# Seven outer products of a Strassen stage: summed in accumulating DMAs instead of on VectorE and GpSimd

## The chip, the cores and the metric

One core of a Trainium2 chip. The metric is device time in microseconds (us) of one execution of the whole program. Five engines work side by side and wait for each other through semaphores: TensorE (PE, with its weight loads as PEld), VectorE (DVE), ScalarE (ACT), GpSimd (POOL) and SyncE (SP, which here only issues DMAs). POOL can issue DMAs as well. Each engine takes its instructions strictly in order: an instruction that waits holds everything behind it on the same engine.

## The reference

Input x has shape (4, 512, 512), all in float32. Two residual blocks follow each other:

```
h = layernorm(x)
i, f, g = h Wi^T, h Wf^T, h Wg^T
gate = sigmoid(f);  v = silu(i) * (1 - gate)
o[t] = gate[t] * o[t-1] + v[t]                     # scan over the 512 tokens
o = o / rms(o) * gnorm_w * g * sigmoid(g)
x = x + layernorm(o Wo)
h = layernorm(x)
hidden = fwht(silu(h W1^T) * (h W3^T))             # width 2048, Walsh-Hadamard
x = x + layernorm(hidden W2^T)
```

The change touches only the last block, the product with W1 and W3, and there only for the batches 2 and 3.

## The kernel before

The Hadamard transform is folded into W2 early in the kernel. Nearly all products are made by one step of Strassen's scheme in Winograd's form: 2x2 blocks, seven products instead of eight. The seven are named P1, P2, P6, P5, P7, P3, P4 in the order in which they are made (`ORDER`, line 33). They go to three PSUM banks: X takes P1, then P6, P7 and P4 on top of it, Y takes P2, Z takes P5 and then P3 on top. Because a bank is summed further, PE may start P6 only when P1 has been read out of X, P7 only after P6 was read, P4 only after P7 was read, and P3 only after P5 was read.

Batches 0 to 3 pass through the attention block, and batches 0 and 1 through the feed-forward block, in this way. The two last batches are treated as a pair (`PAIR = 2, 3`, `ffn_pair`, lines 834 to 914): their product with W1 and W3 gets two levels of the scheme. An outer step stands for one of the seven outer products; it consists of the seven inner products, which I call leaves. A leaf is two matmul calls (line 879) of 128x128 by 128x256 each. The outer order is P1, P2, P6, P7, P5, P4, P3 (`OUTER`). There are four groups g = 0 to 3 of the hidden width, so 4 x 7 outer steps of 7 leaves.

Each leaf is read from PSUM at once (lines 887 to 892), as a 128x512 piece of a 128 x 2048 accumulator in SBUF, `q`, with urgent priority. In the kernel before an outer product is summed as it leaves PSUM. `q0` starts as P1 (ACT copies the fresh pieces, line 889; the other three are added by DVE, line 892); `q1` = q0 + P2, `q0` += P6, `q3` = P7 (fresh pieces again by ACT), `q2` = q0 + P5, all of them by DVE additions that read PSUM. In the step of P5, POOL adds q3 into q0 (line 894) and q2 into q3 (line 896), eight additions of 128x512. Last, q0 += P4 and q2 += P3 by DVE. The four sums are then the four blocks of the result: `hidden` (lines 849 to 865) takes one of them, applies Silu to its first half on ACT (line 852) and multiplies the halves on DVE into the tiles `ht` (line 860, two per call). `combine_left` (lines 158 to 163) then makes the scheme's four sums of each `ht` on POOL.

The product of `ht` with W2, "down" (`ffn_out`, line 684), of one group is made between the leaves of the next group (lines 903 to 907: 56 single matmul calls per group, spread from the fourth leaf to the 48th). The last group's is made after all leaves, in one go, and ends in the normalization and the stores.

What sets the order: PE and SP take their instructions in the order of the source. DVE, ACT and POOL get an order from a scheduler, which goes by priorities and its own estimates; `tc.high_priority` raises a piece of work. `load_leaf_w` (line 813) has SP load the weights of the step three ahead, and POOL makes four sums of them too (`wl`, lines 158 to 163). SP also loads 2 x 896 KB of W2 tiles (`load_down_pair`, line 186) at the start of each group. PSUM has eight banks.

Of the kernel before, what the change touches and what calls it, by code (L numbers as in the profile page):

```python
# [11 lines left out]
F32 = mybir.dt.float32  # L12
AF = mybir.ActivationFunctionType
ALU = mybir.AluOpType
P = 128
# [29 lines left out]
def kernel(  # L45
# [14 lines left out]
    nc = tc.nc  # L60
    B, T, D = x.shape
# [12 lines left out]
    xpool = ctx.enter_context(tc.tile_pool(name="x", bufs=3))  # L74
    stream = ctx.enter_context(tc.tile_pool(name="stream", bufs=5))
    stream2 = ctx.enter_context(tc.tile_pool(name="stream2", bufs=4))
    work = ctx.enter_context(tc.tile_pool(name="work", bufs=1))
# [10 lines left out]
    def bank(name):  # L88
        return psum.tile([P, 2, H], F32, tag="ps", name=name)
# [65 lines left out]
    def combine_left(t, eng, steps=(0, 1)):  # L155

        if 0 in steps:
            eng.tensor_add(t[:, S1], t[:, A21], t[:, A22])  # L158
            eng.tensor_sub(t[:, S2], t[:, S1], t[:, A11])
        if 1 not in steps:  # L160
            return
        eng.tensor_sub(t[:, S3], t[:, A11], t[:, A21])
        return eng.tensor_sub(t[:, S4], t[:, A12], t[:, S2])  # L163
# [85 lines left out]
    def behind(what):  # L249


        return tc.issue_after(read[what].ins)
# [555 lines left out]
        for make, (k, what) in zip(makes, places[first:]):  # L808
            beside.setdefault(k, []).append(partial(step, make, what))

    leaf_w = {}

    def load_leaf_w(n):

        g, k = divmod(n, len(OUTER))
        if g == NU // NS:
            return
        a = OUTER[k][1]
        t = stream.tile([P, 2, 7, P], F32, tag="w", name=f"wl_{g}_{a}")
        for w, name in enumerate(("w1", "w3")):  # L820
            for i in range(NS):
                nc.sync.dma_start(
                    out=t[:, w, 2 * i : 2 * i + 2],
                    in_=saved[name, NS * g + i][:, a].rearrange("p (c f) -> p c f", c=2),
                )
        combine_left(t.rearrange("p w s f -> p s w f"), nc.gpsimd)
        leaf_w[n] = t
# [6 lines left out]
    def ffn_pair(g, down):  # L834

        total, start = len(down), 3
        given = 0
        q = {}
        first_of = {"P1": (0, None), "P7": (3, None), "P2": (1, 0), "P5": (2, 0)}
        to_of = {"P1": 0, "P2": 1, "P6": 0, "P7": 3, "P5": 2, "P4": 0, "P3": 2}  # L840

        def accumulator(k):
            pool, tag, bufs = (work, "d", 2) if k == 0 else (xpool, "x", 3)
            q[k] = pool.tile([P, 2, 2, T], F32, tag=tag, name=f"q{k}_{g}", bufs=bufs)

        def part(k, i, j):
            return q[k][:, :, i, ts(j, H)]

        def hidden(k, h, j):

            d, b = q[k], PAIR[j]
            nc.scalar.activation(d[:, 0], d[:, 0], AF.Silu)  # L852
            for n in range(NS):
                m = NS * g + n
                if (b, m) not in hts:
                    hts[b, m] = work.tile(
                        [P, 7, H], F32, tag="ht", name=f"ht_{b}_{m}", bufs=4
                    )
                t = hts[b, m]
                nc.vector.tensor_mul(  # L860
                    t[:, h : h + 3 : 2],
                    d[:, 0, n].rearrange("p (t f) -> p t f", t=2),
                    d[:, 1, n].rearrange("p (t f) -> p t f", t=2),
                )
            return [hts[b, NS * g + n] for n in range(NS)]

        for step, (outer, _, right, _, _) in enumerate(OUTER):
            load_leaf_w(7 * g + step + AHEAD)
            w, x = leaf_w.pop(7 * g + step), xq[right]
            to, base = to_of[outer], None  # L870
            if outer in first_of:
                to, base = first_of[outer]
                accumulator(to)
            ps = {}
            for s, (what, a, bb, which, first) in enumerate(ORDER):
                if first:
                    ps[which] = bank(f"{which}_u{g}_{step}")
                for k in range(2):
                    nc.tensor.matmul(  # L879
                        ps[which][:, k, :], w[:, k, a, :], x[:, bb, :],  # L880
                        start=first and k == 0, stop=True, skip_group_check=True,
                    )
                i, j = {"P1": (0, 0), "P5": (1, 1), "P6": (0, 1), "P2": (0, 0),
                        "P7": (1, 1), "P3": (0, 1), "P4": (1, 0)}[what]
                fresh = what in ("P1", "P6", "P5", "P4")
                y = part(to, i, j)
                with tc.high_priority(offset=URGENT):
                    if fresh and outer in ("P1", "P7"):
                        read["copy"] = nc.scalar.copy(y, ps[which])  # L889
                    else:  # L890
                        z = part(base, i, j) if fresh and base is not None else y
                        last = nc.vector.tensor_add(y, ps[which], z)  # L892
                if outer == "P5" and fresh:
                    nc.gpsimd.tensor_add(part(0, i, j), part(0, i, j), part(3, i, j))
                if outer == "P5" and what in ("P2", "P7", "P3", "P4"):
                    nc.gpsimd.tensor_add(part(3, i, j), part(3, i, j), part(2, i, j))
                if acts and s in (0, 2, 4):
                    with behind("copy"):
                        acts.popleft()()
                if sums and what in ("P2", "P7", "P3"):  # L900
                    with tc.issue_after(last.ins):
                        sums.popleft()()
                leaf = 7 * step + s + 1
                want = total if leaf >= 48 else total * max(leaf - start, 0) // (48 - start)
                while given < want:
                    down.popleft()()
                    given += 1
            if outer == "P4":
                hidden(1, 0, 0)
                for t in hidden(0, 1, 0):  # L910
                    combine_left(t, nc.gpsimd)
        hidden(3, 1, 1)
        for t in hidden(2, 0, 1):
            combine_left(t, nc.gpsimd)

    def load_wo():
# [304 lines left out]
    for b in range(2):  # L1221
        late = {}
        for m in range(NU):
# [8 lines left out]
            if b == 0 and m in LOW:  # L1232
                p, what, k = LOW[m]
# [56 lines left out]
    for g in range(NU // NS):  # L1290
        load_down_pair(g)
        ffn_pair(g, deque(down))
        down = [
            part
            for b in PAIR
            for part in ffn_out(b, g, True)
        ]
# [36 lines left out]
```

## Time and profile before

| | |
|---|---|
| median of 3 runs | 791.99 us (791.94 to 792.12) |
| the profiled execution | 792.25 us |
| its span in the profile | 790.5 us (so 1.75 us lie around it) |
| PE busy in the span | 776.3 us, 98% |
| DVE, ACT, POOL busy | 564.2, 246.9, 245.5 us |
| granted clock of PE | 0.996 |
| leaves (line 879): first and last matmul record | 490.2 and 755.9 us |
| DVE additions to q (line 892) | 164, mean 0.69 us |
| ACT copies to q (line 889) | 32, mean 0.58 us |
| POOL sums of q (lines 894 and 896) | 32, mean 1.27 us |

The span is the time from the first to the last recorded instruction. A group in the profile is all instructions of one line, engine and operation; the idle time given with it is the engine's own, just before these instructions, with what ended it. The pair stage begins at 490 us, and its four groups at 490, 554, 622 and 690 us; the last "down" runs from 756 to 780 us.

### The profile page before, as it was taken

How to read it: one execution, taken by the hardware profiler on the slowest of the kernel's cores; microseconds unless marked ns; L12 is line 12 of the kernel's file. 1: busy time of each engine (PE TensorE's matmuls, PEld its weight loads, DVE VectorE, ACT ScalarE, POOL GpSimd, SP SyncE). 2: the span in 40 equal slices, each digit the busy share in tenths (PEclk: the TensorE clock that was granted, in tenths of full speed). 3: DMA queues.
4: the chain of work that ended last, by engine and by line, in shares of the span. 5: the costliest groups of instructions: out<-in, count | busy, mean ns of one | idle time of the engine just before them, and what ended most of it. 6: DMA issues, size and time to landing. Idle time of an engine off the chain costs nothing.

```text
span 790.5 us, 10222 instructions
## 1 busy us (share of the span) xinstructions
PE 776.3 (98%) x3608; PEld 670.1 (85%) x3608; DVE 564.2 (71%) x1093; ACT 246.9 (31%) x348; POOL 245.5 (31%) x319
## 2 busy tenths in 40 slices
PE   9999999999999999999999999999999999999994
PEld 7888788888888888888888888888788888888884
DVE  6789889799789774477455459868755655765676
ACT  4374754543436212344223412011321200111112
POOL 2111202112213110001001005088947646672452
PEclk9999999999999999999999999999999999999998
DMA  9997445776997982538246736341521412141012
GB/s 296 398 340 299 156 198 180 218 258 244 339 336 289 340 325 102 160 150 347 94 187 200 267 78 221 131 122 33 195 80 54 157 53 58 49 166 54 1 53 108
DMA packets 78148, 144.93 MB, mean 183 GB/s; under 512 B 6160, under 2 KB 55952, under 8 KB 77712
## 3 DMA queue, kind: packets, MB, share of 16 engines
q1 hardware_dynamic: 68032, 96.82, 38.1%
q0 software_dynamic: 9344, 46.14, 14.9%
q10 hardware_dynamic: 720, 1.31, 0.4%
q8 instruction: 29, 0.48, 0.2%
q14 instruction: 23, 0.19, 0.1%
HBM read 97.06 MB, written 47.19 MB: 182 GB/s over the span
## 4 chain that ended last, share of the span: by engine, by line
PE 88%; DVE 5%; DMA 2%; POOL 1%; issue 1%; SPq 0%; ACT 0%; POOLq 0%; DVEq 0%
PE X_f L517 13%; PE X_po L684 13%; PE X_u L879 11%; PE X_a L517 10%; PE Z_po L684 7%; PE Z_f L517 6%; PE Z_u L879 5%; PE Z_a L517 5%; PE X_y L624 3%; PE Y_f L517 3%; PE Y_po L684 3%; PE Y_a L517 3%; PE Y_u L879 3%; PE Z_y L624 2%; DMA w2p<-in_W_dram 1%
## 5 line engine op out<-in xcount | busy, mean ns | idle before, releaser
L684 PE MATMUL X_po<-w,ht 128*128 128x256 f32 x512 | 132.1, 379 | 0.1
L517 PE MATMUL X_f<-xt_f,w 128*128 128x256 f32 x512 | 121.2, 380 | 0.1
L879 PE MATMUL X_u<-xq,wl 128*128 128x256 f32 x448 | 114.4, 381 | 2.3 <-ACT q L889 0.8
L517 PEld LDWEIGHTS X_f<-xt_f,w 128*128 128x128 f32 x512 | 96.8, 190 | 14.5 <-DVE d_f L492 0.5
L684 PEld LDWEIGHTS X_po<-w,ht 128*128 128x128 f32 x512 | 97.2, 190 | 13.7 <-DVE f L492 0.5
L879 PEld LDWEIGHTS X_u<-xq,wl 128*128 128x128 f32 x448 | 84.2, 190 | 17.1 <-issue 3.6
L892 DVE TENSOR_TENSOR q<-X_u,q 128x512 f32<-128x512 f32 x88 | 60.8, 691 | 42.6 <-PE X_u L879 41.7
L494 ACT COPY d_f<-X_f 128x512 f32<-128x512 f32 x48 | 28.0, 584 | 131.8 <-PE X_f L517 115.7
L684 PE MATMUL Z_po<-w,ht 128*128 128x256 f32 x256 | 66.4, 379 | 0.0
L492 DVE TENSOR_TENSOR f<-X_po,f 128x512 f32<-128x512 f32 x51 | 34.9, 685 | 36.9 <-PE X_po L684 36.9
L517 PE MATMUL Z_f<-xt_f,w 128*128 128x256 f32 x256 | 60.5, 379 | 0.0
L879 PE MATMUL Z_u<-xq,wl 128*128 128x256 f32 x224 | 57.6, 379 | 0.0
L684 PEld LDWEIGHTS Z_po<-w,ht 128*128 128x128 f32 x256 | 48.6, 190 | 6.8 <-DVE f L492 0.2
L517 PEld LDWEIGHTS Z_f<-xt_f,w 128*128 128x128 f32 x256 | 48.6, 190 | 6.6
L263 POOL TENSOR_TENSOR rs_f<-rs_f,power 128x2 f32<-128x2 f32 x16 | 13.4, 840 | 117.8 <-DVE nm_f L364 73.5
L852 ACT ACTIVATE q<-q 128x1024 f32<-128x1024 f32 x16 | 16.9, 1057 | 103.8 <-DVE q L892 58.2
L879 PEld LDWEIGHTS Z_u<-xq,wl 128*128 128x128 f32 x224 | 42.5, 190 | 6.0 <-DVE q L892 0.3
L892 DVE TENSOR_TENSOR q<-Z_u,q 128x512 f32<-128x512 f32 x48 | 33.1, 689 | 20.1 <-PE Z_u L879 19.5
L158 POOL TENSOR_TENSOR wl<-wl 128x256 f32<-128x256 f32 x28 | 21.3, 762 | 77.4 <-DMA wl<-s_w 70.2
L494 ACT COPY d_a<-X_a 128x512 f32<-128x512 f32 x36 | 21.1, 585 | 67.8 <-PE X_a L517 67.6
L889 ACT COPY q<-X_u 128x512 f32<-128x512 f32 x24 | 14.0, 584 | 89.4 <-PE X_u L879 76.8
L179 POOL DMA_DIRECT2D s_w<-w x24 | 13.1, 547 | 72.5 <-DVE w L163 56.9
(205 smaller groups left out, 1459.2 us busy)
## 6 DMA issues: line engine op xcount, KB each, us to landing
w<-s_w SPq DMA_DIRECT2D x32, 896.0 KB, 6.4
s_w<-w POOLq DMA_DIRECT2D x24, 896.0 KB, 6.9
wl<-s_w SPq DMA_DIRECT2D x112, 128.0 KB, 2.7
w<-in_W_dram SPq DMA_DIRECT2D x32, 256.0 KB, 6.4
wi<-s_wi SPq DMA_DIRECT2D x6, 896.0 KB, 9.3
wf<-s_wf SPq DMA_DIRECT2D x6, 896.0 KB, 5.4
wg<-s_wg SPq DMA_DIRECT2D x6, 896.0 KB, 6.3
w_h<-w2p POOLq DMA_DIRECT2D x8, 512.0 KB, 5.7
```

The source lines that it names most:

```text
L158: eng.tensor_add(t[:, S1], t[:, A21], t[:, A22])
L179: nc.gpsimd.dma_start(out=saved[key], in_=t)
L263: read["power"] = nc.gpsimd.tensor_tensor(r, r, power_t[:, 0:n], ALU.pow)
L492: read[what] = nc.vector.tensor_add(to, ps[which], to)
L494: read["copy"] = nc.scalar.copy(to, ps[which])
L517: nc.tensor.matmul(ps[:, n, :], w[:, a, c, :], xt[:, bb, c, :], start=first and n == 0 and c == 0, stop=c == 1, skip_group_check=True,)
L624: nc.tensor.matmul(ps[:, t, :], og[:, a, c, ts(t, P)], w[c][:, bb, :], start=first and t == 0 and c == 0, stop=c == 1, skip_group_check=True,)
L684: nc.tensor.matmul(ps[:, t, :], hts[b, m][:, a, ts(t, P)], w[m][:, W2[bb], :], start=first and k == 0, stop=m == ms[-1], skip_group_check= ...
L852: nc.scalar.activation(d[:, 0], d[:, 0], AF.Silu)
L879: nc.tensor.matmul(ps[which][:, k, :], w[:, k, a, :], x[:, bb, :], start=first and k == 0, stop=True, skip_group_check=True,)
L889: read["copy"] = nc.scalar.copy(y, ps[which])
L892: last = nc.vector.tensor_add(y, ps[which], z)
```

## The change

Every outer product but P3 is now written fresh to an accumulator of its own: ACT copies the four fresh leaves (P1, P6, P5, P4), DVE adds the other three onto them. P3 is added by DVE onto the buffer called q0, all seven leaves. There are five accumulators, allocated once, whose parts rotate between groups (`places`). The sums between accumulators are six DMAs per group (`gather`), issued by POOL with `accum_op=add`: each adds one whole accumulator of 128 x 2048 float32 (1 MB) to another in SBUF. In the notation "target += source" they are: q1 += q0 after P2's step, q0 += q4 after P6's, q3 += q0 after P7's, q0 += q2 and then q2 += q3 after P5's, q3 += q4 after P4's. The POOL additions of lines 894 and 896 are gone. `hidden` is called for q1 after P5's step, for q2 and q3 after P4's, and for q0 at the end. In the changed kernel the gather is line 849, Silu 866, the product into `ht` 874, the leaf's matmul 890, the ACT copy 900 and the DVE addition 902.

```diff
-        q = {}
-        first_of = {"P1": (0, None), "P7": (3, None), "P2": (1, 0), "P5": (2, 0)}
-        to_of = {"P1": 0, "P2": 1, "P6": 0, "P7": 3, "P5": 2, "P4": 0, "P3": 2}
-
-        def accumulator(k):
-            pool, tag, bufs = (work, "d", 2) if k == 0 else (xpool, "x", 3)
-            q[k] = pool.tile([P, 2, 2, T], F32, tag=tag, name=f"q{k}_{g}", bufs=bufs)
+        roles = {"P1": 0, "P2": 1, "P6": 4, "P7": 3, "P5": 2, "P4": 4, "P3": 0}
+        places = {0: 1, 1: 4, 4: 3, 3: 2, 2: 0}
+        if not q:
+            for k in range(5):
+                pool, tag, bufs = (work, "d", 2) if k in (0, 4) else (xpool, "x", 3)
+                q[k] = pool.tile([P, 2, 2, T], F32, tag=tag, name=f"q{k}", bufs=bufs)
+        else:
+            before = dict(q)
+            q.update({k: before[place] for k, place in places.items()})
+
+        def gather(to, part):
+            nc.gpsimd.dma_start(
+                out=q[to].rearrange("p n i t -> p (n i t)"),
+                in_=q[part].rearrange("p n i t -> p (n i t)"),
+                accum_op=ALU.add,
+            )
+
+        gathers = {
+            "P2": ((1, 0),), "P6": ((0, 4),), "P7": ((3, 0),), "P5": ((0, 2), (2, 3)),
+            "P4": ((3, 4),),
+        }
...
-            to, base = to_of[outer], None
-            if outer in first_of:
-                to, base = first_of[outer]
-                accumulator(to)
+            to = roles[outer]
...
-                    if fresh and outer in ("P1", "P7"):
+                    if fresh and outer != "P3":
                         read["copy"] = nc.scalar.copy(y, ps[which])
                     else:
-                        z = part(base, i, j) if fresh and base is not None else y
-                        last = nc.vector.tensor_add(y, ps[which], z)
-                if outer == "P5" and fresh:
-                    nc.gpsimd.tensor_add(part(0, i, j), part(0, i, j), part(3, i, j))
-                if outer == "P5" and what in ("P2", "P7", "P3", "P4"):
-                    nc.gpsimd.tensor_add(part(3, i, j), part(3, i, j), part(2, i, j))
+                        last = nc.vector.tensor_add(y, ps[which], y)
...
+            for pair in gathers.get(outer, ()):
+                gather(*pair)
+            if outer == "P5":
+                hidden(1, 0, 0)
             if outer == "P4":
-                hidden(1, 0, 0)
-                for t in hidden(0, 1, 0):
+                hidden(2, 1, 1)
+                for t in hidden(3, 1, 0):
                     combine_left(t, nc.gpsimd)
-        hidden(3, 1, 1)
-        for t in hidden(2, 0, 1):
+        for t in hidden(0, 0, 1):
             combine_left(t, nc.gpsimd)
```

More of the change, by code (lines that the diff above doesn't have):

```diff
@@ L809, in pair_beside @@
             beside.setdefault(k, []).append(partial(step, make, what))
-    leaf_w = {}
+    leaf_w, q = {}, {}
     def load_leaf_w(n):
```

## The prediction

> **What bounds the kernel now.** I read the page's busy times first, then its chain that ended last.
>
> ```profile
> span 790.5 us, 10222 instructions
> PE 776.3 (98%) x3608; PEld 670.1 (85%) x3608; DVE 564.2 (71%) x1093; ACT 246.9 (31%) x348; POOL 245.5 (31%) x319
> PE 88%; DVE 5%; DMA 2%; POOL 1%; issue 1%; SPq 0%; ACT 0%; POOLq 0%; DVEq 0%
> ```
>
> PE is the path. Whether anything the change relieves holds PE up is seen in the table of stretches, cut at the four groups of the pair stage (columns: stretch, its length, then busy time and instructions of PE, PEld, DVE, ACT and POOL, granted clock, DMA share, GB/s).
>
> ```profile
> 490.00:554.00 64.00, 63.10 (x287) 53.54 (x286) 50.59 (x82) 8.24 (x12) 41.09 (x48) 1.00 0.29 91
> 554.00:622.00 68.00, 67.32 (x310) 58.20 (x309) 42.74 (x69) 15.63 (x24) 47.50 (x60) 1.00 0.30 94
> 622.00:690.00 68.00, 67.22 (x312) 58.89 (x311) 41.62 (x64) 8.80 (x12) 41.95 (x52) 1.00 0.27 83
> 690.00:756.00 66.00, 66.00 (x307) 57.84 (x306) 40.92 (x63) 8.81 (x12) 33.11 (x40) 1.00 0.21 75
> ```
>
> PE is idle 0.90 + 0.68 + 0.78 + 0 = 2.4 us in the whole stage. That is about all that any relief of DVE and POOL can win. The waits of PE name 0.8 us for ACT's q and 0.5 us for DVE's q, those of PEld 1.7 us more for DVE's q, part of it beneath running matmuls.
>
> **What goes and what comes, by count.** Away: DVE additions of line 892 fall from 164 to 25 a group (three in each of six steps, seven in P3's), 100 in all: 64 x 0.69 = 44 us less on DVE. The POOL sums go: 32 x 1.27 = 41 us. Added: 64 ACT copies x 0.58 = 37 us, and 24 gathers, whose issue takes POOL some 0.55 us each (the row of its stores of the output), 13 us. All of this lies beside PE: ACT goes from 8.8 to about 18 of 66 us in a group. I count the sum as 0, and at best 2.2 us won. An ACT copy is also no slower than the addition it replaces (0.58 against 0.69), so PSUM banks come free no later while ACT's queue flows.
>
> **What the gathers cost is a chain of waits.** Take G as the time from the issue of one gather to the earliest issue of one that waits for it. In a group, q0 += q2, then q2 += q3, then q3 += q4 must follow one another: the second writes what the first reads, the third writes what the second reads. The first can go only when P5's step is read out. POOL waits in front of each, with `wl` and `ht` sums queued behind. Then Silu needs q3. I lay this on the trace of before, since PE's order of work is unchanged.
>
> ```profile
> 601.22 1.03 PE L879 MATMUL X_u<-xq,wl 128*128 128x256 f32 x4
> 621.08 1.89 PE L879 MATMUL X_u<-xq,wl 128*128 128x256 f32 x8
> 624.62 1.10 PE L879 MATMUL X_u<-xq,wl 128*128 128x256 f32 x4 [0.79 <-ACT q L889]
> ```
>
> These are PE's rows: the last leaf of group 1's P5 step, the last of its P3 step (first half of the 8), and a wait that is there already.
>
> *Groups 1, 2 and 3.* P5's last leaf ends at 602.25; ACT's copy (0.09 us later, 0.58 us) ends at 602.9; the first gather issues at 603.0 and the third lands at 603.0 + 3G. In the built program the first `ht` product of that block (line 874) stands in DVE's queue between P3's Z addition and P7's X addition. So DVE waits for the landing and Silu (1.06, line 852's row), multiplies (0.69), adds P7 (0.69), with 0.2 for hand-overs, and behind it wait the rest of the leaf additions, and PE, whose P4 leaf was due at 621.0: stall 603.0 + 3G + 2.6 - 621.0 = 3G - 15.4. The P4 gather's own input is ready at about 613, before 603 + 2G.
>
> *Group 0* has shorter steps. P5's last leaf ends at 537.4, first gather 538.1; here Silu stands in ACT's queue ahead of the copy of the next group's P1, and P6 of that step was due at 555.8: stall 538.1 + 3G + 1.06 + 0.58 + 0.2 - 555.8 = 3G - 15.9.
>
> *A second place* in groups 1 to 3: Silu of q1 stands in ACT's queue after P6's copy in step 3 of the group (outer P6), ahead of P5's copy, and waits for q1 += q0. In group 1 P2's step is read out at 573.6; Silu and copy with hand-overs add 1.8; P3's leaf, which sums onto P5's bank, is due at 580.0: stall G - 4.6. In group 0 Silu stands one copy later, where no leaf of that bank follows: 0.
>
> Sum: (3G - 15.9) + 3(3G - 15.4) + 3(G - 4.6), no term below 0.
>
> **G is not in the trace**; no DMA there adds. Three rows bound it, minimum, median and maximum from issue to landing: 256 KB stores from POOL (line 724), 896 KB stores (179), 1 MB loads (151), and the page's row of POOL's queue.
>
> ```profile
> DMA to landing us min/median/max: 2.0/3.4/7.5
> DMA to landing us min/median/max: 3.9/7.4/12.6
> DMA to landing us min/median/max: 4.7/4.9/5.0
> q0 software_dynamic: 9344, 46.14, 14.9%
> ```
>
> 46.14 MB in 14.9% of 790.5 us is 392 GB/s while packets run, so 1.05 MB takes 2.7 us and 256 KB 0.67; the fixed part is 2.0 - 0.67 = 1.33 us (check: 896 KB gives 3.7, the row's minimum is 3.9). From below: the addition is free, landing 4.0, G = 4.1. From above: two reads and a write one after the other, 1.33 + 3 x 2.7 = 9.4, G = 9.5. I take two transfers' worth, since source and target must both be read while the write can run beside them: 1.33 + 5.4 = 6.7, with 0.15 for POOL to wake, G = 6.9. It is also between the quiet (4.0) and the loaded (7.4, 896 KB median) rows.
>
> The Trainium skill, "Collectives: The Full Stack", the bandwidth ceiling in Part 3, speaks against this change: an add in the DMA costs no cycles, but needs two source reads, and halves the rate (62.28 against 32.35 GB/s, a ratio of 1.93). No run here shows it yet; with 1.93 in place of 2 the landing would be 6.5 and the stall some 3 us less. Its praise of such sums, that compute engines stay free, is what the table above makes worthless here: they are not the path.
>
> With G = 6.9: 4.8 + 3 x 5.3 + 3 x 2.3 = 27.6 us. The forecast is 792.25 + 27.6 = 819.9, say 820 (made against the profiled execution, which stands 0.26 above the median of its three runs). With G = 6 it would be 14, with G = 8.2 about 47: its own range is 806 to 840.
>
> Other waits I cost at nothing: POOL's `wl` sums behind the gathers. In group 1 with G = 6.9 POOL is through with both waits and 16 `ht` sums of some 0.76 us by about 36 us after P5's end, while the weights that follow are needed some 50 us after it (a stalled PE needs them later still). If that cover went, POOL's four sums (3 us) would come on top, three times.
>
> **Rivals.**
> 1. *Not slower: the gather is as quick as a plain transfer.* G = 4.1: 3G = 12.3 is under 15.4, and 4.1 under 4.6, so every stall is 0 and the cover of two steps holds. It decides at G = 4.6 (second place) and 5.1 (group ends). Then the relieved DVE and ACT's earlier P1 copy can give back up to 2.2 us: 790 to 792.3. For it: POOL's quiet stores are that quick. Against: a second read. That also is the case in which the change does not do what it says: the engines are freed, and nobody waited for them.
> 2. *Reads and writes one after the other*, G = 9.5: 12.6 + 3 x 13.1 + 3 x 4.9 = 66.6, and since G exceeds group 0's steps (8.2 us), its six gathers chain from P2's step on, 3.4 more: 862. For it: 896 KB stores took up to 12.6 us.
> 3. *G = 6.9, but the third gather meets the W2 loads*, which SP issued at 552.0, 620.8 and 688.3, the ends of the groups. 2 x 896 KB at 392 GB/s hold the engines 4.7 us: up to 3 x 4.7 = 14 more, 834.
>
> **Numbers.** Forecast 0.50, rival 1 0.22, rival 2 0.18, rival 3 0.10. 0.2% is 1.6 us, about what a measurement of this kernel can tell from no change. Of rival 1's 0.22 I give 0.15 to faster and 0.07 to the same; slower has 0.78. The range takes in both ends of G, 790 to 862, because rivals 1 and 2 hold 0.4 together and only slower DMAs yet (some 0.1) may be left out.
>
> **What would show it.** Right: landing of line 849 at 6 to 8 us; PE idle of 4 to 7 us at each group's end, released by DVE's line 902 or ACT's 900 behind Silu (866) and a DMA; some 2 us in each P6 step of groups 1 to 3; DVE and POOL less busy by about 44 and 28 us. Wrong: landing under 4.6 us, PE idle at 2 us as before (rival 1); landing over 9 and POOL waiting for one gather after the other through the whole group (rival 2); only the third gather long (rival 3). Wholly wrong would be PE waiting for `wl`, or ACT's added copies holding PE with no DMA behind them.

## The result and the profile after

The changed kernel takes 866.88 us (median of 4 runs, 865.41 to 868.53) against 792.06 us of the kernel before in the same batch (4 runs): a ratio of 1.0944, 95% interval 1.0919 to 1.0968. It is slower, as forecast, but by 75 us and not by 28; the time lies above the range of 790 to 862. The profiled execution took 868.53 us, 1.8 us of it outside the span.

The page of the changed kernel: busy times, the queue of POOL's DMAs (the gathers among them), shares of the chain that ended last, and the two DMA groups that matter (KB of one, median us from issue to landing).

```profile
span 866.7 us, 10251 instructions
PE 794.4 (92%) x3608; PEld 682.5 (79%) x3608; DVE 527.7 (61%) x1029; ACT 284.0 (33%) x412; POOL 230.2 (27%) x311
...
q0 software_dynamic: 12800, 71.31, 28.2%
...
PE 68%; DMA 19%; DVE 5%; issue 3%; POOL 2%; ACT 1%; SPq 1%; POOLq 0%; DVEq 0%; ACTq 0%
...
q<-q POOLq DMA_DIRECT2D x24, 1024.0 KB, 7.7
...
wl<-s_w SPq DMA_DIRECT2D x112, 128.0 KB, 2.9
```

DMA now holds 19% of the chain, where it held 2%. Two sums place the loss. The span grew by 76.2 us. PE's idle time grew from 790.5 - 776.3 = 14.2 to 866.7 - 794.4 = 72.3 us, by 58.1. PE's busy time grew by 18.1 with the same 3608 matmuls. So three quarters of the loss are waits, and one quarter is the same matmuls running slower.

The table of stretches of the changed kernel, each cut at the end of the wait that closes a group (columns as in the prediction: stretch, length, PE, PEld, DVE, ACT, POOL, granted clock, DMA share, GB/s):

```profile
490.00:572.88 82.88, 67.72 (x296) 57.12 (x294) 42.05 (x70) 19.34 (x32) 32.57 (x41) 0.91 0.69 174
572.88:666.79 93.91, 70.10 (x297) 59.81 (x297) 31.45 (x46) 22.88 (x37) 41.02 (x55) 0.86 0.55 135
666.79:750.95 84.16, 70.67 (x309) 60.85 (x309) 31.87 (x47) 18.08 (x28) 38.57 (x51) 0.93 0.57 134
750.95:831.62 80.67, 71.25 (x308) 61.34 (x308) 31.42 (x48) 18.08 (x28) 29.14 (x39) 0.92 0.51 118
```

The stretches are 80.7 to 93.9 us long, where those of before had 64 to 68 (cut some leaves apart from these). PE is idle 9 to 24 us in each, and the granted clock, 1.00 in all four before, is 0.86 to 0.93. DVE is relieved, by 564.2 - 527.7 = 36.5 us, and POOL by 15.3 (44 and 28 were forecast: a gather's issue holds POOL 0.87 us and not 0.55, and the products into `ht` and their sums take somewhat longer than before). That is worth nothing, since PE waits for something else. The timeline of PE in the changed kernel names it. Only its rows behind a wait of more than 2.7 us are shown; in brackets stands the idle time ahead of the matmuls and what ended it:

```profile
552.24 2.05 PE L890 MATMUL X_u<-xq,wl 128*128 128x256 f32 x4 [3.33 <-DVE q L902]
572.88 2.04 PE L890 MATMUL X_u<-xq,wl 128*128 128x256 f32 x4 [10.13 <-ACT q L900]
607.51 2.07 PE L890 MATMUL Z_u<-xq,wl 128*128 128x256 f32 x4 [5.80 <-ACT q L900]
666.79 3.78 PE L890 MATMUL X_u<-xq,wl 128*128 128x256 f32 x8 [15.41 <-DVE q L902]
697.62 1.62 PE L890 MATMUL Z_u<-xq,wl 128*128 128x256 f32 x4 [3.12 <-ACT q L900]
750.95 3.78 PE L890 MATMUL X_u<-xq,wl 128*128 128x256 f32 x8 [10.37 <-DVE q L902]
782.05 1.13 PE L890 MATMUL Z_u<-xq,wl 128*128 128x256 f32 x4 [2.82 <-ACT q L900]
831.62 2.07 PE L890 MATMUL X_u<-xq,wl 128*128 128x256 f32 x4 [6.61 <-DVE q L902]
```

The waits of 10.13, 15.41, 10.37 and 6.61 are the four group ends, 42.5 us. The three of Z_u (5.80, 3.12, 2.82) are the P6 steps, 11.7 us. Both were forecast as places. The wait of 3.33, and two more of 1.49 and 2.60, 7.4 us together, were not. The second column shows the other quarter of the loss: four matmuls took 1.03 or 1.10 us in the rows of before, and 2.04 to 2.07 us in four of these rows.

What stands behind the longest wait is seen on POOL in the changed kernel. The first row of this timeline is the first gather of group 1's end, the last row the third:

```profile
633.30 0.88 POOL L849 DMA_DIRECT2D q<-q  x1 [4.13 <-ACT q L900]
641.55 0.72 POOL L158 TENSOR_TENSOR wl<-wl 128x256 f32<-128x256 f32 x1 [7.36 <-DMA wl<-s_w]
...
643.71 0.73 POOL L163 TENSOR_TENSOR wl<-wl 128x256 f32<-128x256 f32 x1
644.39 0.86 POOL L849 DMA_DIRECT2D q<-q  x1
652.65 0.86 POOL L849 DMA_DIRECT2D q<-q  x1 [7.41 <-DMA q<-q]
```

And on ACT, the Silu that waits for the third gather:

```profile
664.35 1.06 ACT L866 ACTIVATE q<-q 128x1024 f32<-128x1024 f32 x1 [11.19 <-DMA q<-q]
```

From the first issue to the Silu it is 664.35 - 633.30 = 31.05 us, where the prediction had 3 x 6.9 = 20.7. Two things lengthen it. The scheduler put four sums of `wl` between the first gather and the second; they wait for a weight load of 128 KB that travels beside the gather and lands 7.6 us after its issue at 633.8, where the median is 2.9. It lands with the gather; of the 11.1 us from the first issue to the second, 7.9 are the gather itself and 2.8 the sums behind it. And the third gather takes 664.35 - 652.65 = 11.7 us to land. The spread over all 24 is in the answer for line 849:

```profile
DMA to landing us min/median/max: 6.9/7.7/12.1
```

### The profile page after: what moved, and what is told of

Read it like the earlier page. It is cut to its first block, busy times and chain, and to the rows that moved or that the text cites. A ratio compares the mean times of both kernels' runs of the same rounds, so it can differ in the third digit from the quotient of the medians.

```text
span 866.7 us, 10251 instructions
## 1 busy us (share of the span) xinstructions
PE 794.4 (92%) x3608; PEld 682.5 (79%) x3608; DVE 527.7 (61%) x1029; ACT 284.0 (33%) x412; POOL 230.2 (27%) x311
## 4 chain that ended last, share of the span: by engine, by line
PE 68%; DMA 19%; DVE 5%; issue 3%; POOL 2%; ACT 1%; SPq 1%; POOLq 0%; DVEq 0%; ACTq 0%
DMA q<-q 15%; PE X_f L517 12%; PE X_a L517 9%; PE X_po L684 9%; PE Z_f L517 6%; PE X_u L890 5%; PE Z_a L517 5%; PE Z_po L684 4%; DMA wl<-s_w 3%; PE X_y L624 3%; PE Y_f L517 3%; PE Z_u L890 3%; PE Y_a L517 2%; PE Y_po L684 2%; PE Z_y L624 2%
## 5 line engine op out<-in xcount | busy, mean ns | idle before, releaser
L890 PE MATMUL X_u<-xq,wl 128*128 128x256 f32 x448 | 124.4, 407 | 50.1 <-DVE q L902 38.3
L890 PEld LDWEIGHTS X_u<-xq,wl 128*128 128x128 f32 x448 | 91.0, 205 | 67.4 <-DVE q L902 37.1
L684 PE MATMUL X_po<-w,ht 128*128 128x256 f32 x512 | 134.6, 385 | 0.1
L684 PEld LDWEIGHTS X_po<-w,ht 128*128 128x128 f32 x512 | 99.1, 194 | 14.6 <-DVE f L492 0.5
L900 ACT COPY q<-X_u 128x512 f32<-128x512 f32 x72 | 42.1, 586 | 153.9 <-PE X_u L890 133.9
L890 PE MATMUL Z_u<-xq,wl 128*128 128x256 f32 x224 | 61.0, 397 | 11.7 <-ACT q L900 11.7
L890 PEld LDWEIGHTS Z_u<-xq,wl 128*128 128x128 f32 x224 | 44.1, 198 | 19.2 <-ACT q L900 12.9
L902 DVE TENSOR_TENSOR q<-X_u,q 128x512 f32<-128x512 f32 x40 | 27.6, 689 | 51.1 <-PE X_u L890 23.4
L874 DVE TENSOR_TENSOR ht<-q 128x512 f32<-128x512 f32 x32 | 27.4, 869 | 48.2 <-ACT q L866 41.9
L684 PEld LDWEIGHTS Z_po<-w,ht 128*128 128x128 f32 x256 | 49.7, 195 | 7.3 <-DVE f L492 0.2
L517 PEld LDWEIGHTS Z_f<-xt_f,w 128*128 128x128 f32 x256 | 48.6, 190 | 6.6
L902 DVE TENSOR_TENSOR q<-Y_u,q 128x512 f32<-128x512 f32 x28 | 19.3, 689 | 54.5 <-PE Y_u L890 45.8
L849 POOL DMA_DIRECT2D q<-q x24 | 21.0, 874 | 115.9 <-ACT q L900 59.4
```

The costliest lines, as they stand in the source:

```text
L517: nc.tensor.matmul(ps[:, n, :], w[:, a, c, :], xt[:, bb, c, :], start=first and n == 0 and c == 0, stop=c == 1, skip_group_check=True,)
L684: nc.tensor.matmul(ps[:, t, :], hts[b, m][:, a, ts(t, P)], w[m][:, W2[bb], :], start=first and k == 0, stop=m == ms[-1], skip_group_check= ...
L849: nc.gpsimd.dma_start(out=q[to].rearrange("p n i t -> p (n i t)"), in_=q[part].rearrange("p n i t -> p (n i t)"), accum_op=ALU.add,)
L874: nc.vector.tensor_mul(t[:, h : h + 3 : 2], d[:, 0, n].rearrange("p (t f) -> p t f", t=2), d[:, 1, n].rearrange("p (t f) -> p t f", t=2),)
L890: nc.tensor.matmul(ps[which][:, k, :], w[:, k, a, :], x[:, bb, :], start=first and k == 0, stop=True, skip_group_check=True,)
L902: last = nc.vector.tensor_add(y, ps[which], y)
```

## The experiments

Each was timed in turns with the kernel before on one chip; ratios are against that. What is open after the trace: how much belongs to the addition inside the DMA, how much to the places in the queues, and why matmuls after a wait are slow.

**1. Small gathers.** Everything of the change stays, but each gather carries an eighth of the accumulator.

```diff
-                out=q[to].rearrange("p n i t -> p (n i t)"),
-                in_=q[part].rearrange("p n i t -> p (n i t)"),
+                out=q[to].rearrange("p n i t -> p (n i t)")[:, 0:256],
+                in_=q[part].rearrange("p n i t -> p (n i t)")[:, 0:256],
```

> Each gather adds only 256 of the 2048 columns (128 KB); the other columns of the five accumulators are left unsummed. Order, copies, additions and waits stay. Theory 1 (the time went into the length of the gathers, by the chain of waits behind them): landing 2 to 2.6 us in place of 7.7, each wait under its cover, PE idle in the leaves 2 to 4 us in place of 62, PE busy back at about 776 us, time 789 to 795 us. Theory 2 (the added ACT copies, the new places of Silu and of the products into ht in the queues cost by themselves, however short the DMAs): 815 us or more, PE waiting for ACT and DVE with no DMA behind them.

Measured: 794.53 us, 1.0039 (1.0026 to 1.0051). The page of that kernel, and its answer for line 849:

```profile
PE 777.1 (98%) x3608; PEld 671.3 (85%) x3608; DVE 522.9 (66%) x1029; ACT 283.5 (36%) x412; POOL 225.7 (28%) x311
```

```profile
DMA to landing us min/median/max: 2.6/2.7/7.1
```

With landings of 2.7 us 72 of the 75 us are gone, and PE's busy time is back within 0.8 us of before. So the added ACT copies, the new order and the issues on POOL cost 2.8 us at most; the duration of the gathers costs. It also shows the gain from the relief by itself: DVE has 41 us less to do than before and the kernel is not faster.

**2. Plain copies.** The gathers keep their size and drop the addition.

```diff
-                accum_op=ALU.add,
```

> The gathers are plain copies of the same 1 MB from SBUF to SBUF, without the addition (so sums are missing). Theory 1, with the second read as its price: landing about 5 us in place of 7.7; 2.7 us less per gather make 3 x 2.7 less at each of four group ends and 2.7 less at three second places, 40 us, and some 10 us of the lost clock come back: 812 to 825 us. Rival (reads and writes inside SBUF are slow, addition or not): landing stays at 7 us or more and the time at 855 to 868 us.

Measured: 815.39 us, 1.0294 (1.0279 to 1.031). The answer for its gathers' line:

```profile
DMA to landing us min/median/max: 4.5/4.7/9.3
```

The addition costs 2.4 us of landing at the minimum, 3.0 in the median, and 866.88 - 815.39 = 51 us of the kernel. The plain transfer still costs 24. Its longest wait, 7.56 us, is the end of group 0, where the third copy lands after 9.3 us. Rival 1 was priced at nothing; here G is 5.2 (626.86 to 632.07 us, two issues of group 1), for which the prediction's sum gives 2.4 us, and 24 came. So the forecast's terms were too few even there: in group 0 four `wl` sums, after a wait of 5.25 us for their load, hold the second copy back, just as above.

**3. W2 loads away from the group's end.** They are issued in step 3 of the group instead (counted from 0).

```diff
+            if step == 3:
+                load_down_pair(g)
...
-        load_down_pair(g)
```

> The changed kernel with one edit: SP issues the two 896 KB loads of W2 tiles in the fourth step of each group and not ahead of its first. Theory 1 with the collision (the third gather takes 12 us because it shares the DMA engines with these loads): its landing falls to 7 to 8 us, 4.3 us less at three group ends, 13 us, and a little clock: 848 to 855 us. Rival (the third gather is long for a reason of its own, or what waits next is as late): its landing stays near 12, or the time stays at 863 to 870 us.

Measured: 860.89 us, 1.0874 (1.0858 to 1.089). The third landings of groups 0 to 2 fell from 12.1, 11.7 and 9.3 us to 8.3, 6.9 and 6.9, about as expected (the longest of all gathers is now 10.0), and the group ends' waits to 8.97, 9.79, 8.24 and 6.12, that is 33.1 instead of 42.5 us. The time fell by only 6 us, half of what was expected at least. The collision is real, and it isn't the main term.

**4. Sums of `wl` behind the third gather**, in the P3 step only.

```diff
-        combine_left(t.rearrange("p w s f -> p s w f"), nc.gpsimd)
+        with ExitStack() as order:
+            if behind_gather is not None:
+                order.enter_context(tc.issue_after(behind_gather.ins))
+            combine_left(t.rearrange("p w s f -> p s w f"), nc.gpsimd)
...
-            load_leaf_w(7 * g + step + AHEAD)
+            load_leaf_w(7 * g + step + AHEAD, gathered if outer == "P3" else None)
```

> The changed kernel with one edit: the POOL sums of the weights that are loaded in the P3 step are put behind the third gather; they stood between the first and the second gather of P5's step, and waited there for their load. Theory 1 with POOL's queue as a part: in groups 1 and 2 the second gather follows the first after 7.5 to 8.3 us in place of 11, so 2 x 3 = 6 us less and a little clock: 856 to 862 us. Rival (the weights then come too late, PE waits for wl): 866 us or more, with PE idle released by POOL's wl.

Measured: 859.65 us (856.41 to 864.81), 1.0863 (1.0822 to 1.0903). The profile is of the longest execution, 864.81. The timeline of POOL in this kernel, same place as above:

```profile
631.29 0.88 POOL L852 DMA_DIRECT2D q<-q  x1 [4.19 <-ACT q L903]
639.18 0.86 POOL L852 DMA_DIRECT2D q<-q  x1 [7.01 <-DMA q<-q]
646.70 0.86 POOL L852 DMA_DIRECT2D q<-q  x1 [6.67 <-DVE q L905]
647.27 1.06 POOL L158 TENSOR_TENSOR wl<-wl 128x256 f32<-128x256 f32 x1
```

The three gathers now follow each other directly, from first to third issue in 15.4 us instead of 19.35, and the wait of PE behind them fell from 15.41 to 7.97. Group 2's grew from 10.37 to 15.06 in this execution, with a landing of 13.3 us there. By the medians the time fell by 7 us, within the expectation. The sums of `wl` were a cost, as seen; that their absence moves the chain's end into other traffic is argued from the one landing, not shown.

**5 and 6. Silu and products behind the leaf reads.** In the changed kernel ACT and DVE wait for the last gathers with leaf copies queued behind. Experiment 6 defers only that work, into the next group's first two steps, behind a copy and an addition of that place; experiment 5 does this with the edits of 3 and 4.

```diff
-                hidden(1, 0, 0)
-            if outer == "P4":
-                hidden(2, 1, 1)
-                for t in hidden(3, 1, 0):
-                    combine_left(t, nc.gpsimd)
-        for t in hidden(0, 0, 1):
-            combine_left(t, nc.gpsimd)
+                late(copied, last, q[1], g, 0, 0)()
+        waiting.extend(
+            (late, q[k], g, h, j) for k, h, j in ((3, 1, 0), (2, 1, 1), (0, 0, 1))
+        )
...
+                if waiting and (step, s) in ((0, 5), (1, 3), (1, 5)):
+                    make, *what = waiting.pop(0)
+                    make(copied, last, *what)()
```

(`late` makes `hidden`, and its sums, under `tc.issue_after` of the copy and the addition given to it; the last group's are made at its end.)

> The changed kernel with only the third of these edits, the later Silu and products; the W2 loads and the weight sums on POOL stay where they were. Theory 1: the third gather lands as late as before, up to 31 us after P5's step; what waits for it is due some 10 us later than before, so the two long waits at the group ends shrink to 5 us or less each, the waits in the P6 steps go, and the last group's stays: 808 to 825 us. Rival (what waits next is due as soon): 850 us or more.

> The changed kernel with the two edits of the third and fourth run, and a third: Silu of a finished block and its products into ht stand behind the leaf copies and additions; those of q3, q2 and q0 are made in the first two steps of the next group, when their sums have landed (in the last group behind its last leaf). The six gathers and their chain stay. Theory 1 (a gather costs what PE has to wait for behind Silu and the products, not what it takes): no wait at three of four group ends nor in the P6 steps, a wait of 5 to 8 us before the last product with W2, and 2 us of clock: 798 to 808 us. Rival (24 MB added in the DMAs cost by contention, or the copies by themselves): 820 us or more, with PE idle that no third gather releases.

Measured: experiment 6 takes 833.75 us, 1.0515 (1.049 to 1.054), experiment 5 819.99 us (817.49 to 824.03), 1.0355 (1.0322 to 1.0388). Both miss their expectations, by 9 and 12 us, to the slow side. Still, the place of Silu and the products alone is worth 33 us, more than any other edit: the gathers are as long as before (median 7.4 us), and fewer instructions queue behind them. What is left in experiment 5 is a wait of 5.16 us before the last product with W2, which was expected, and 8.6 us in group 0, which were not:

```profile
553.16 2.00 PE L905 MATMUL X_u<-xq,wl 128*128 128x256 f32 x4 [4.70 <-DVE q L917]
571.30 2.07 PE L905 MATMUL X_u<-xq,wl 128*128 128x256 f32 x4 [3.92 <-DVE q L917]
```

The 4.70 is the wait of P3's additions: DVE must add them onto q0, and q0 += q2 is still on its way. It is the same place as the 3.33 at 552.24 in the changed kernel, which the prediction didn't list.

**7. Keeping PE at work.** Spare products of the identity, 24 to 60 in a row, stand before the four leaves that waited longest; no result uses them. Theory A says that PE's clock falls while it waits and takes time to come back; theory B that the gathers' traffic slows the matmuls.

```diff
+                spare = {(1, 6, 6): 60, (2, 6, 6): 42, (3, 6, 6): 24, (1, 0, 2): 38}
+                if (g, step, s) in spare:
+                    p = psum.tile([P, P], F32, tag="ps", name=f"warm_{g}_{step}")
+                    for _ in range(spare[g, step, s]):
+                        nc.tensor.matmul(p, ident, ident, start=True, stop=True)
```

> The changed kernel with spare matmuls (identity by identity, to a bank of their own, read by nobody) in front of the four leaves that wait at the group ends: 38, 60, 42 and 24 of them, some 0.22 us each, so 8, 13, 9 and 5 us, a little less than the waits there. Theory A (after an idle time of 3 us or more the granted clock drops and the next 3 to 6 us of matmuls run at half speed, 2 to 3 us lost each): the matmuls after these waits take 0.86 us per leaf again, 857 to 862 us. Theory B (they are slow for another reason, or the spare matmuls push the rest): 866 to 875 us.

Measured: 869.51 us, 1.0986 (1.0957 to 1.1015). Two rows of PE's timeline in this kernel:

```profile
555.23 2.05 PE L895 MATMUL X_u<-xq,wl 128*128 128x256 f32 x4 [6.83 <-DVE q L907]
576.03 1.10 PE L895 MATMUL X_u<-xq,wl 128*128 128x256 f32 x4 [1.92 <-ACT q L905]
```

Behind the spare products the matmuls at 576.03 ran at 1.10 us, where they had taken 2.04; other waits, such as the 6.83, still ended slow. The time did not fall to the 857 to 862 us that theory A stood for. It speaks for A in the row and not in the time. The clock wasn't kept up as a whole: waits of 2.23 and 2.55 us were left at two of the group ends and ended slow, and PE still worked 30.9 us at a granted clock of 0.50, against 36.1 in the changed kernel. So this run doesn't measure what a full clock is worth.

**8. Halves.** Each gather is two DMAs of half an accumulator.

```diff
-            nc.gpsimd.dma_start(
-                out=q[to].rearrange("p n i t -> p (n i t)"),
-                in_=q[part].rearrange("p n i t -> p (n i t)"),
-                accum_op=ALU.add,
-            )
+            for n in range(2):
+                nc.gpsimd.dma_start(
+                    out=q[to][:, n].rearrange("p i t -> p (i t)"),
+                    in_=q[part][:, n].rearrange("p i t -> p (i t)"),
+                    accum_op=ALU.add,
+                )
```

> The changed kernel with each gather as two DMAs of half the columns (512 KB each), so that the second half of one and the first half of the next can run together. Theory 1, transfers bound by the DMA engines' packets (5.4 us of 7.2): three sums in a row take 18 to 19 us in place of 22, some 3 us less at four group ends: 850 to 857 us. Rival (the fixed part counts twice, POOL issues twice as often): 864 to 875 us.

Measured: 845.36 us, 1.0678 (1.066 to 1.0695), 21.5 us less than the changed kernel and better than expected. A half lands in 5.8 us (median, 4.5 at least) where a whole takes 7.7, and the group ends' waits are 6.11, 5.25, 5.65 and 4.38. From first issue to last landing the chains take 26.6, 20.0, 20.4 and 19.2 us, where 18 to 19 were expected. Group 1's is the one that shrank most, by 11 us, and there the `wl` sums no longer wait for their load between two gathers; how much of the gain is that change of place, and how much the halves themselves, isn't separated.

**9 and 10. Waits without gathers.** The kernel before, with no DMA added: ACT reads a fresh leaf several times over. Experiment 9 reads 6 times more in six steps, for short waits; experiment 10 reads 17 times more in two steps, for two long ones.

```diff
+                        if what == "P1" and (g, outer) in [(1, "P2"), (2, "P2")]:
+                            for _ in range(17):
+                                nc.scalar.copy(y, ps[which])
```

> The kernel before, with six short idle times made for PE on purpose: in six outer steps (P2, P7 and P5 of groups 1 and 2) ACT reads the first leaf out of PSUM six times over (6 x 0.58 us) before it is read as before, so that the third leaf waits some 2 to 3 us. No DMA is added. Theory A (the clock drops only after waits longer than about 3 us): the time grows by the idle time and by little more, 12 to 18 us, and PE's busy time stays within 2 us of 776. Theory B (every wait costs clock): PE busy up by 8 us or more.

> The kernel before, with two long idle times made for PE in the same way: in the P2 steps of groups 1 and 2 ACT reads the first leaf 17 times over (9.9 us), so that the third leaf waits some 8 to 9 us each time. Theory A: the matmuls right after each wait run at about half speed for some 3 to 6 us, PE busy grows by 4 to 6 us, and the time by the idle time plus that, 21 to 25 us. Theory B (matmuls after the waits of the changed kernel were slow for the sake of its DMAs or its accumulators): PE busy stays at 776 and the time grows by the idle time alone, 16 to 19 us.

Measured: experiment 10 takes 816.09 us, 1.0298 (1.0283 to 1.0314), experiment 9 815.99 us (813.09 to 817.79), 1.0296 (1.0272 to 1.0319), where 12 to 18 us more were expected and 24 came. The timeline of PE in experiment 10 behind its first wait, and the table of stretches there:

```profile
575.49 2.04 PE L879 MATMUL X_u<-xq,wl 128*128 128x256 f32 x4 [9.97 <-DVE q L895]
...
580.29 1.03 PE L879 MATMUL X_u<-xq,wl 128*128 128x256 f32 x4
```

```profile
575.40:580.30 4.90, 4.81 (x13) 3.92 (x14) 3.63 (x6) 0.00 (x0) 0.81 (x2) 0.55 0.15 57
580.30:585.20 4.90, 4.90 (x24) 4.33 (x23) 2.52 (x4) 0.69 (x2) 0.31 (x1) 1.00 0.14 54
```

In the 4.9 us after the wait PE does 13 matmuls at a granted clock of 0.55, in the next 4.9 us 24 at 1.00, and DMAs are as little busy in both (0.15 and 0.14). No gather is there. So theory B falls: it is the wait that slows what follows it. Two waits of 9.97 and 9.26 us cost 780.3 - 776.3 = 4.0 us of PE's busy time, 2.0 each, beside their own length.

In experiment 9 PE's busy time grew by 4.3 us, between the two theories (2 at most, 8 or more). Its matmuls were slow after two waits of 2.74 us, and not after waits of 2.85, 3.21 and 3.31. So length alone doesn't decide. The traces show what does: in every profiled run the granted clock is 1.00 or 0.50 and changes only at times that lie a multiple of 3.41 us apart (here at 591.42, 594.84, 669.93 and 673.34 us). In the table of experiment 9 the wait of 3.31 falls into the first two rows, one of the waits of 2.74 into the third:

```profile
564.12:567.53 3.41, 1.70 (x8) 1.14 (x6) 0.00 (x0) 3.31 (x7) 3.33 (x6) 1.00 0.41 117
567.53:570.94 3.41, 1.81 (x9) 1.63 (x10) 2.54 (x4) 0.70 (x2) 3.33 (x5) 1.00 0.02 5
588.01:591.42 3.41, 0.79 (x4) 0.36 (x2) 0.69 (x1) 3.22 (x6) 1.65 (x3) 1.00 0.25 73
591.42:594.84 3.42, 3.30 (x8) 2.71 (x9) 0.69 (x1) 0.58 (x1) 1.16 (x2) 0.50 0.00 0
```

The wait of 3.31 is split: PE is idle 1.71 and 1.60 us of two such stretches, and the clock stays. The wait of 2.74 lies almost whole in one stretch, 2.62 us, and the clock halves at its end. Between 480 and 785 us of the profiled runs, stretches at full clock were followed by half clock where PE was idle in them for 2.0 us or more, and not at 1.98 or less, with one exception (1.87 us, in experiment 7).

**11. All that helped** (5 and 8 together).

> The changed kernel with all the edits that helped: W2 loads in the fourth step, POOL's weight sums behind the third gather, Silu and products later, and each gather as two DMAs of half the columns. Theory 1: the wait before the last product with W2 shrinks by some 3 us against the run without the halves, group 0's waits by as much, a little clock with them: 805 to 814 us. Rival (twice the issues on POOL take it back): 818 us or more. In either case not under 794, the time with gathers of an eighth.

Measured: 807.53 us (806.04 to 809.13), 1.0189 (1.017 to 1.0209), within the expectation. The longest wait of PE left, 3.56 us, is now before the last products with W2, for late `ht`, as is one of 2.31; group 0 keeps waits of 2.17 and 2.80. No version with gathers beat the kernel before.

## Why the prediction was right in sign and wrong in size

**Right: what is relieved wins nothing.** 41 us less on DVE brought no gain (experiment 1), as PE's 2.4 idle us in the whole stage had told.

**Right: the mechanism and its places.** PE waits at the four group ends and in the P6 steps of groups 1 to 3, behind Silu, behind a gather. A quiet landing was sized well, 6.7 us against 6.9 at least, though the row it came from was misread: the 2.0 us of line 724 is a store that SP issued, POOL's own took 2.4 at least. The frame of the group-end formula held too: set the measured chains, 26.9, 31.05, 25.0 and 22.25 us from the first issue to Silu, in the place of 3G, and "3G - 15.9" and "3G - 15.4" give 11.0, 15.65, 9.6 and 6.85; measured are 10.13, 15.41, 10.37 and 6.61.

**The step that failed: "With G = 6.9: 4.8 + 3 x 5.3 + 3 x 2.3 = 27.6 us".** Two faults: G was used three times over, as if each gather of the chain had the quiet duration and nothing stood between them, and a term is missing. Term by term, on the profiled execution, which lies 868.5 - 819.9 = 48.6 us above the forecast:

- *Group ends*: 42.5 instead of 20.7, 21.8 us more. The chains are 105.2 us together instead of 82.8. Of the 22.4, 12.5 are the third landings: 12.1, 11.7, 9.3 and 7.0 us instead of 6.9. That is rival 3, which had up to 14; group 3, where no W2 loads run, is the 7.0, and experiment 3 brought the others down. It was no rival: it came with the forecast and ought to have been a term of it. Another 4.2 are the hop from the first issue to the second in group 1, 11.1 us instead of 6.9; 2.8 of them are the `wl` sums, which the prediction had cleared: "Other waits I cost at nothing". They were counted behind the gathers, not between them. The last 5.7 are the other seven hops, each somewhat longer than 6.9: 7.2 is the shortest (806.94 to 814.14 us, in group 3).
- *P6 steps*: 11.7 instead of 6.9, 4.8 more. Most of it is group 1's, 5.80 instead of 2.3: ACT's last copy of P2's step ended at 595.0, but q1 += q0 was issued only at 598.45, because POOL was busy without a break from 574.14 on, with sums of `ht` and `wl` and with stores; those sums had themselves waited 11.49 us for group 0's late `ht`. That too was among the waits costed at nothing.
- *Places not listed*: 7.4 us, of which 3.33 is P3's addition onto q0. The 2.60 goes back to the same full POOL queue: DVE waited 4.15 us for a small operation of POOL (`rs_f`, line 263) ahead of its addition.
- *The clock*, 18.1 us: no term at all. The waits slow the matmuls after them. After eight of the ten waits above PE works for a while at half clock. These are the first and the third of the eight stretches, from the wait's end (or the fall of the clock, where that comes later) to the clock's return, and the sum over all eight:

```profile
552.24:558.17 5.93, 5.93 (x14) 4.76 (x15) 3.46 (x10) 0.00 (x0) 0.22 (x1) 0.50 0.88 177
607.51:612.79 5.28, 5.28 (x13) 4.20 (x14) 2.05 (x3) 0.00 (x0) 0.00 (x0) 0.50 0.00 2
sum 36.06, PE 36.05 PEld 28.84 DVE 22.53 ACT 4.16 POOL 16.74; mean PE 4.51 PEld 3.60 DVE 2.82 ACT 0.52 POOL 2.09
```

At half clock 36.05 us hold the work of 18.0, so the clock accounts for the whole 18.1, 2.3 us for each of the eight waits. In the second row the DMAs are idle and the clock is 0.50 all the same. What one would gain by keeping the clock up stays open (experiment 7).

21.8 + 4.8 + 7.4 + 18.1 = 52.1; less the 2.4 us idle before that the forecast left in its base, 49.7, against 48.6.

The Trainium skill, "TensorE: Matmul & The Clock Gate", Part 1, would have warned of the clock: an idle window of about 3.4 us halves the rate, and a busy window of about 3.4 us restores it. From it one estimates 3.4/2 = 1.7 us for each wait; experiment 10 measured 2.0, and the changed kernel 2.3. The page also says that the window runs freely. The traces agree on its length, 3.41 us, and on that; but a window need not be idle as a whole, 2.0 us of it sufficed here. With seven predicted waits the measured price would have added at most 7 x 2.0 = 14 us to the forecast, less if some of the three waits of 2.3 us were split.

The other page's ratio came near. For the second source read ("Collectives: The Full Stack", the bandwidth ceiling in Part 3, a ratio of 1.93), take the prediction's fixed 1.33 us, an estimate, from both landings: (7.7 - 1.33) / (4.7 - 1.33) = 1.89 in the median, (6.9 - 1.33) / (4.5 - 1.33) = 1.76 at the minimum. So rival 2, one after the other with G = 9.5, is no case of quiet transfers, though its time, 862, is nearest to the measured one: that is luck, the way there was another.

## What to carry to other kernels

A DMA that takes over a sum moves work off engines, and is worth something only where those engines end the path; look for their waits on the bounding engine first. A chain of dependent DMAs is to be priced with the traffic that runs at that very time and with all that stands between two issues on the issuing queue, not as a multiple of a quiet landing. And each new wait of PE costs its length and, here, about 2 us more of slow matmuls; work that must wait for a DMA belongs behind the reads that PE needs (33 us here).

## What the runs showed of the hardware that was not expected

- An accumulating DMA of 1 MB from SBUF to SBUF lands in 6.9 us at least, the plain copy in 4.5; its issue held POOL for 0.86 us, the plain copy's for 0.57 (experiment 2).
- A 128 KB load beside such a gather needed 7.6 us, with a median of 2.9 over all. (In the kernel before the longest of them, beside the loads of W2, took 7.4.)
- PE's matmuls ran at half speed for 4.3 us after a wait of 10 us (575.49 to 579.82 us in experiment 10), with no added DMA near, and were slow after some waits as short as 2.74 us. The granted clock changed only at times a multiple of 3.41 us apart, so that where a wait fell decided as much as how long it was.
